# Preparing the last layers' weights inside a row scan, folding a norm into message weights, and moving stores and columns to the scalar queue

## The chip, the cores and the metric

The kernel runs on one core of a Trainium2 chip. A core has a matrix engine (TensorE, PE in the profile; PEld is its weight load), a vector engine (DVE), a scalar engine (ACT), GpSimd (POOL) and SyncE (SP), which here gives out most of the DMAs. Each engine takes its instructions in order; a DMA is given out by SP or ACT (SPq and ACTq in a timeline) and moved by the core's 16 DMA engines. The metric is device time of one execution in microseconds (us); lower is better.

## What is computed

The input is x of 4 images (b), 128 channels, 128x128 positions, all in fp32. Four layers follow each other, each as `x = x + layer(gn(x))`, with `gn` a group norm over 32 groups of 4 channels. Cut to what matters here:

```python
# layer 0: deformable 3x3 convolution, relu
x = x + relu(deform_conv(gn(x), offset))
# layer 1: scan over rows; conv1d over 9 taps of the row before
def step(carry, row):
    new = row + relu(conv1d_same(carry, W))
    return new, new
x = x + scan(step, gn(x))
# layer 2: messages along rows and columns
v = gn(x)
x = x + v @ Wself.T + (sum(v, axis=2) @ Wm.T)[:, :, None] + (sum(v, axis=1) @ Wk.T)[:, None]
# layer 3: triangle product with gates
xn = layer_norm(gn(x), norm_g, norm_b)
left = (xn @ left_w + left_b) * sigmoid(xn @ lgate_w + lgate_b)
right = (xn @ right_w + right_b) * sigmoid(xn @ rgate_w + rgate_b)
out = einsum('bkjd,bkid->bijd', left, right)
out = layer_norm(out, onorm_g, onorm_b) * sigmoid(xn @ ogate_w + ogate_b)
x = x + (out @ to_out_w + to_out_b)
```

## The kernel before

The kernel is one program of four stages. The first, `deform_layer`, is not touched by the change; it ends by writing x1 (the input of layer 1) to DRAM.

**Weights of the last layers** (`last_weights`, called ahead of the scan). Five columns, the output weights and the five matrices of layer 3 (left, right and their gates, 512 columns in all, and the output gate's 128) are loaded on ACT's queue, their biases on SP's. From them `wcat` is made: the matrices times the norm's gain (`gained`), with two matmuls for each of two pieces (512 and 128 columns), in PSUM tiles `prep_ps` and `prepb_ps` of a pool of their own, and copies by DVE (lines 1206 to 1218). After it the kernel loads the message layer's three matrices on ACT's queue.

**Scan** (`scan_layer`). Rows are handled in groups of RB = 4; the four images share each instruction where they can. For each row y and each half h of the images there are eight matmuls `both_ps` (L1099), one and eight more `own_ps` (L1104, L1110), then on ACT a copy `shared` and on DVE `total`, `carry` (the new row), `diff` and `x2c` (the row of layer 1's output). The next row's input is transposed by PE (`x1T_ps`, L1064) and normed by ACT (`rowT`). `own_ps` comes from a pool of 3 buffers. At the end of a group DVE takes statistics of `x2c` (`bn_stats`, L1144) and its sum over w (`sum_w`, L1148), POOL adds `sum_h`, and ACT's queue stores x2T. Input rows are loaded on SP (`x1rows`), the scan's own weights `wconv` on ACT's queue. Tile's scheduler orders the instructions of each engine in this and all earlier stages.

**Message terms** (`message_terms`). From the statistics come s and t, so that gn(x2) = s x2 + t. The self term is folded into one matrix per image, `ws` = wself s + identity. The sums over w and over h (128x512 for all images) are normed by four DVE operations `msg`, multiplied by wm and wk, and wself t is added by a third product; `z` of shape (2, image, 128) is the row term and the column term.

**Last layers** (`last_layers`), image by image, with an order written out by hand: `manual_schedule` keeps the instructions of each engine in the order of the program, and generators are advanced by `step`. For image b:
- `messages(b)`: for eight rows of positions at a time, `x2c` is loaded, `pair_ps` = ws x2c (L1345), `zc` = row term + column term (POOL, L1332), and X = pair_ps + zc (DVE, L1349), with statistics.
- `scaled(b)`: the scale `s` of X (L1380) and a matrix `cs`; X is stored as `x3T` in eight stores of 1 MB (L1375), for the residual at the end.
- `normed(b)`: `pair_ps` = cs X (L1435), its square `sq` on ACT (L1441), and X rewritten on ACT; from the squares `divided` makes the standard deviation, sends it through DRAM (`stdT`, `rstd`, `rwide`, all on SP's queue) and multiplies X by it.
- `multiplied(b, q)` for four quarters q of the hidden columns: left and right times their gates, the output gates stored as `gateT`, then the triangle product into `T`.
- `given_out(b)`: 32 steps k of four columns. A step loads `x3` (from x3T) and `gate` (from gateT) on SP's queue, transposes `u` (L1585), makes y on ACT (L1587), multiplies it by the gate (L1588, on POOL, and on DVE for the last image), multiplies by the output weights (L1600), and copies the sum to `x` on ACT (L1617), which SP stores. `u`, the normed column of T, is made two steps ahead: of a step's four columns three on ACT (L1615) and one on POOL (L1613); for the last image, whose output has nothing beside it, two and two.

`given_out(b-1)` is `out_of` in the main loop: its steps stand among those of image b's messages, `scaled`, `normed` and first three quarters. While it passes the three steps of `scaled` it is at k = 2, 3 and 4.

Of the kernel before, what the change touches and what calls it, by code (L numbers as in the profile page):

```python
# [10 lines left out]
F32 = mybir.dt.float32  # L11
I32 = mybir.dt.int32
BF16 = mybir.dt.bfloat16
AF = mybir.ActivationFunctionType
ALU = mybir.AluOpType
AX = mybir.AxisListType
PSUM = bass.MemoryType.PSUM
DRAM = bass.MemoryType.DRAM

P = 128  # L20
B = 4
S = 128
# [985 lines left out]
                nc.vector.tensor_copy(to, v)  # L1008


def scan_layer(tc, c, small, x1, w, norms, x2T):

# [6 lines left out]
    nc = tc.nc  # L1019
    RB = 4  # L1020
# [9 lines left out]
    with ExitStack() as ctx:  # L1030
# [54 lines left out]
        diffs = [None, None]  # L1085
        for y in range(S):
            i = y % RB
            if i == 0:
                x2c = two.tile([P, B, RB, S], F32, name="x2c")
                if y + RB < S:  # L1090
                    chunks[y + RB] = rows(y + RB)
            px, rt = ready.pop(y)
            old, new = carry[(y + 1) % 2], carry[y % 2]
            conv = []
            if y:
                for h in range(2):
                    both = ps_b.tile([P, HB, V], F32, name="both_ps")
                    for j in range(NJ):
                        nc.tensor.matmul(  # L1099
                            both, lhsT=wsum[:, j, :], rhs=old[h][:, 1, :, j : j + V],  # L1100
                            start=(j == 0), stop=(j == NJ - 1),
                        )
                    own = ps_y.tile([P, 2, HB, V], F32, name="own_ps")
                    nc.tensor.matmul(  # L1104
                        own, lhsT=wt[:, TAPS - 1, :], rhs=old[h][:, :, :, NJ : NJ + V],
                        start=True, stop=False,
                    )
                    for n in range(2):
                        for j in range(NJ):
                            nc.tensor.matmul(  # L1110
                                own[:, n], lhsT=wt[:, 2 * j + n, :],
                                rhs=diffs[h][:, n, :, j : j + V],
                                start=False, stop=(n == 1 and j == NJ - 1),
                            )
                    conv.append((both, own))
            if y + 1 < S:
                ready[y + 1] = turned(chunks[(y + 1) // RB * RB], (y + 1) % RB)
            for h in range(2):
                bs = slice(h * HB, (h + 1) * HB)
                mid = new[h][:, :, :, PAD // 2 : PAD // 2 + V]  # L1120
                if y:
                    both, own = conv[h]
                    shared = two.tile([P, HB, V], F32, name="shared")
                    nc.scalar.copy(shared, both)
                    total = two.tile([P, 2, HB, V], F32, name="total")
                    nc.vector.tensor_tensor(
                        total, own, shared.unsqueeze(1).to_broadcast([P, 2, HB, V]), ALU.add
                    )
# [12 lines left out]
            if i == RB - 1:  # L1141
                y0 = y + 1 - RB
                for b in range(B):
                    nc.vector.bn_stats(  # L1144
                        stats[:, b, y // RB, :], x2c[:, b].rearrange("p h w -> p (h w)")
                    )
                    nc.scalar.dma_start(x2T[b, :, y0 : y + 1, :], x2c[:, b])
                nc.vector.tensor_reduce(sum_w[:, :, y0 : y + 1], x2c, AX.X, ALU.add)  # L1148
                for r in range(RB):
                    nc.gpsimd.tensor_tensor(sum_h, sum_h, x2c[:, :, r], ALU.add)  # L1150
                chunks.pop(y0)
    return stats, sum_w, sum_h


def last_weights(tc, c, wp, w3):

    nc = tc.nc
    (norm_g, norm_b, left_w, left_b, right_w, right_b, lgate_w, lgate_b, rgate_w, rgate_b,
# [21 lines left out]
    NP_ = NQ * 4 * DQ + P  # L1180
    wcat = w.wcat = wp.tile([P, NP_], F32, name="wcat")
    w.gcols = slice(NQ * 4 * DQ, NP_)
    with tc.tile_pool(name="l3prep", bufs=1) as prep, tc.tile_pool(
        name="l3ps_w", bufs=2, space=PSUM
    ) as ps_w:
        raw = prep.tile([P, NP_], F32, name="wraw")
        braw = prep.tile([1, NP_], F32, name="braw")
        blocks = raw[:, 0 : NQ * 4 * DQ].rearrange("p (q n e) -> p q n e", q=NQ, n=4)
# [15 lines left out]
        nc.vector.tensor_scalar(less[0:1], less[0:1], -1.0, None, ALU.add)  # L1204
        for n0 in range(0, NP_, 512):
            n1 = min(n0 + 512, NP_)
            pw = ps_w.tile([P, 512], F32, name="prep_ps")
            nc.tensor.matmul(
                pw[:, : n1 - n0], lhsT=less, rhs=gained[:, n0:n1], start=True, stop=True
            )  # L1210
            nc.vector.tensor_copy(wcat[:, n0:n1], pw[:, : n1 - n0])
            pb = ps_w.tile([P, 512], F32, name="prepb_ps")
            nc.tensor.matmul(
                pb[:, : n1 - n0], lhsT=bwide, rhs=raw[:, n0:n1], start=True, stop=True
            )
            nc.vector.tensor_tensor(
                wcat[0:1, n0:n1], pb[0:1, : n1 - n0], braw[:, n0:n1], ALU.add
            )
    return w


def message_terms(tc, c, keep, work, counted, w2, outb):


    nc = tc.nc
    stats, sum_w, sum_h = counted
    wself, wm, wk = w2
    ws = keep.tile([P, B, P], F32, name="ws")
    z = keep.tile([P, 2, B, S], F32, name="z")
    with tc.tile_pool(name="l2ps", bufs=1, space=PSUM) as psum:  # L1230
# [15 lines left out]
        nc.vector.reciprocal(s, s)  # L1246
        t = work.tile([P, B], F32, name="t2")
        nc.vector.scalar_tensor_tensor(t, mean, -1.0, s, ALU.mult, ALU.mult)
        for b in range(B):
            nc.vector.scalar_tensor_tensor(  # L1250
                ws[:, b], wself, s[:, b : b + 1], c.ident, ALU.mult, ALU.add
            )
        tsum = work.tile([P, B], F32, name="tsum")
        nc.vector.tensor_scalar(tsum, t, float(S), None, ALU.mult)
        msg = work.tile([P, 2, B, S], F32, name="msg")
        for n, sums in enumerate((sum_w, sum_h)):
            for by, op in ((s, ALU.mult), (tsum, ALU.add)):
                nc.vector.tensor_tensor(
                    msg[:, n], sums if op is ALU.mult else msg[:, n],
                    by.unsqueeze(2).to_broadcast([P, B, S]), op,  # L1260
                )
        twide = work.tile([P, B, S], F32, name="twide")
        nc.vector.tensor_copy(twide, t.unsqueeze(2).to_broadcast([P, B, S]))
        pm = psum.tile([P, B, S], F32, name="row_ps")
        nc.tensor.matmul(pm, lhsT=wm, rhs=msg[:, 0], start=True, stop=False)
        nc.tensor.matmul(pm, lhsT=wself, rhs=twide, start=False, stop=True)
        pk = psum.tile([P, B, S], F32, name="column_ps")
        nc.tensor.matmul(pk, lhsT=wk, rhs=msg[:, 1], start=True, stop=True)

        nc.vector.tensor_scalar(z[:, 0], pm, outb, None, ALU.add)  # L1270
        nc.scalar.copy(z[:, 1], pk)
    return ws, z


def last_layers(tc, c, terms, w, x2T, out, x3T, gateT, stdT):
# [9 lines left out]
    with ExitStack() as ctx:  # L1285
# [74 lines left out]
        def scaled(b):  # L1360
# [11 lines left out]
            nc.vector.tensor_tensor(d, d, d, ALU.mult)  # L1372
            nc.vector.tensor_tensor(d, d, mv[:, 1:2], ALU.add)
            for j0 in range(0, S, 16):
                nc.sync.dma_start(x3T[b, :, j0 : j0 + 16, :], X[:, j0 : j0 + 16, :])  # L1375
# [153 lines left out]
        def given_out(b):  # L1529
# [45 lines left out]
            for k in range(-6, NS_ + 1):  # L1575
# [31 lines left out]
                if 0 <= k + 2 < NS_:  # L1607
                    u = us[k + 2] = two.tile([P, 4, P], F32, name="u")
                    for j, (r, m) in enumerate(factors.pop(k + 2)):
                        of = column(b, 4 * (k + 2) + j)  # L1610
                        to = u[:, j].rearrange("p (q d) -> p q d", q=NQ)
                        if j >= (2 if alone else 3):
                            nc.gpsimd.tensor_scalar(to, of, r, m, ALU.mult, ALU.add)  # L1613
                        else:
                            nc.scalar.activation(to, of, AF.Identity, bias=m, scale=r)  # L1615
# [62 lines left out]
def tile_preact_convs(ctx: ExitStack, tc: tile.TileContext, x, w_off, b_off, w_def, w_conv,  # L1678
# [17 lines left out]
    with tc.If(nc.values_load(far, min_val=0, max_val=1) > 0):  # L1696
        deform_general(tc, c, norms, x, w_off, b_off, w_def, x1, imgs)
    wp = ctx.enter_context(tc.tile_pool(name="l3w", bufs=1))
    w = last_weights(tc, c, wp, w3)
    with tc.tile_pool(name="l2", bufs=1) as l2:  # L1700
        w2 = []
        for v, name in ((wself_T, "wself"), (wm_T, "wm"), (wk_T, "wk")):
            t = l2.tile([P, P], F32, name=name)
            nc.scalar.dma_start(t, v)
            w2.append(t)
        counted = scan_layer(tc, c, l2, x1, w_conv, norms, x2T)
# [50 lines left out]
```

## Time and profile before

| | us |
|---|---|
| median of 3 runs | 5461.79 |
| lowest, highest | 5455.35, 5473.43 |
| the profiled execution | 5459.8 |
| its span | 5458.1 |
| first stage (to the scan's start) | 3088 |
| scan | 3088 to 3956 |
| message terms | 3956 to 3973 |
| last layers | 3973 to 5458 |

The mean granted clock of TensorE is 0.960. The stages are read from the timeline by the first and last instruction of their lines. Image 0 of the last layers takes 3973 to 4262, each later one some 360, and the last output alone, without other work, 116 us at the end.

A row of a timeline reads: start in the span, time, engine, line, operation, the tile written <- the tiles read, shape, how often in a row, and in brackets how long the engine had been idle and what ended that. SPq and ACTq are the times in which a queue's engine gave out a transfer. A row of waits reads: engine, operation and line, what it waited for, then us in total, times, and the longest. A row of the windows gives, after its length, the busy time of PE, PEld, DVE, ACT and POOL, the granted clock, the share of the DMA engines and the GB/s.

### The profile page before, as it was taken

Reading aid. Unit: us, or ns where it says so; the run is one execution under the profiler, and the core shown is the slowest. Engines: PE = TensorE matmul, PEld = TensorE weight load, DVE = VectorE, ACT = ScalarE, POOL = GpSimd, SP = SyncE. Lnnn points to the kernel's source line nnn. Section 1 sums busy time; section 2 is a strip of 40 time slices with the busy share of each in tenths; the row PEclk is TensorE's granted clock in tenths of the full one; section 3 lists DMA queues with packets and bytes.
Section 4 is the critical chain, followed back from the end, with each engine's and each line's share of the span. In section 5 each row is a group of like instructions: output and inputs, shape, how many; then the busy total and the mean of one; then the engine's idle time right before and its main releaser. Section 6 shows DMA issues by size and latency. Waiting matters only on the chain. (4 is left out here: it accounts for less than half of the span.)

```text
span 5458.1 us, 162832 instructions
## 1 busy us (share of the span) xinstructions
PE 4887.5 (90%) x68890; PEld 4229.0 (77%) x68890; DVE 3237.4 (59%) x8389; ACT 2536.8 (46%) x5206; POOL 1137.0 (21%) x1013
## 2 busy tenths in 40 slices
PE   1898999999999998989999799999969699798897
PEld 1787788788888787877899699999928478396596
DVE  4676666666666655665545466666654654546445
ACT  1554454544554444545544233333234375573666
POOL 4222121210221201212100011111120232323222
PEclk9999998999999999999999899999989899899998
DMA  5776666665666665665644322222141553554535
GB/s 151 162 161 145 138 139 140 142 150 103 142 138 130 157 120 107 150 130 126 129 85 90 73 82 78 78 84 83 61 166 64 174 179 122 195 172 145 191 132 193
DMA packets 1273817, 710.67 MB, mean 130 GB/s; under 512 B 845645, under 2 KB 1112174, under 8 KB 1263862
## 3 DMA queue, kind: packets, MB, share of 16 engines
q1 hardware_dynamic: 1243538, 658.56, 47.8%
q10 hardware_dynamic: 29540, 41.60, 2.2%
q8 instruction: 545, 8.93, 0.7%
q14 instruction: 194, 1.59, 0.1%
HBM read 417.28 MB, written 282.55 MB: 128 GB/s over the span
## 5 line engine op out<-in xcount | busy, mean ns | idle before, releaser
L606 PE MATMUL conv_ps<-ring,wdef 128*128 128x192 f32 (+2 forms) x7632 | 1301.2, 320 | 8.7 <-DVE x1c L576 6.6
L514 DVE TENSOR_TENSOR m<-t_ps,tent 128x390 f32<-128x390 f32 x1548 | 806.7, 557 | 783.2 <-ACT tent L512 767.5
L606 PEld LDWEIGHTS conv_ps<-ring,wdef 128*128 128x128 f32 x7632 | 1146.9, 195 | 127.1 <-issue 64.6
L512 ACT COPY tent<-t_ps 128x390 f32<-128x390 f32 x1560 | 690.5, 487 | 654.7 <-PE t_ps L498 642.2
L498 PE MATMUL t_ps<-parts_of,spread 57*64 57x99 bf16 (+1 forms) x12384 | 742.5, 275 | 169.0 <-DVE m L514 149.3
L523 PE MATMUL v_ps<-m,pixels 60*64 60x108 f32 (+1 forms) x22704 | 812.5, 264 | 19.0 <-DVE m L514 11.1
L498 PEld LDWEIGHTS <-spread 57*64 57x64 bf16 x12480 | 578.7, 125 | 313.0 <-issue 265.7
L523 PEld LDWEIGHTS v_ps<-m,pixels 60*64 60x64 f32 x22704 | 673.0, 137 | 69.8 <-DVE m L514 24.7
L549 ACT COPY ring<-v_ps 128x432 f32<-128x432 f32 x1032 | 505.1, 525 | 445.7 <-PE v_ps L523 444.8
L420 POOL TENSOR_TENSOR off<-off,koff 72x512 f32<-72x512 f32 x128 | 162.7, 1271 | 1768.2 <-DVE off L417 1768.2
L1500 DVE TENSOR_TENSOR T<-pair_ps,sig 128x256 f32<-128x256 f32 x512 | 282.6, 594 | 390.8 <-ACT sig L1497 390.7
L1110 PEld LDWEIGHTS own_ps<-diff,wconv 128*128 128x128 f32 x4064 | 493.6, 191 | 13.1
L1492 PEld LDWEIGHTS pair_ps<-wcat,X 128*128 128x128 f32 x4096 | 472.7, 192 | 38.1 <-issue 29.1
L1110 PE MATMUL own_ps<-diff,wconv 128*128 128x128 f32 x4064 | 494.6, 273 | 0.0
L1492 PE MATMUL pair_ps<-wcat,X 128*128 128x128 f32 x4096 | 481.5, 276 | 5.2 <-DVE T L1500 3.1
L506 PE MATMUL t_ps<-parts_of,spread 57*64 57x130 bf16 x9288 | 454.5, 225 | 0.0
L1150 POOL TENSOR_TENSOR sum_h<-sum_h,x2c 128x512 f32<-128x512 f32 x128 | 162.4, 1268 | 1150.5 <-DVE x2c L1136 684.8
L438 DVE SCALAR_TENSOR_TENSOR parts<-off,parts 72x512 bf16<-72x512 f32 x384 | 296.1, 771 | 153.5 <-ACT parts L430 147.7
L1068 ACT ACTIVATE rowT<-x1T_ps,t_x,s_x 128x128 f32<-128x128 f32 x512 | 208.2, 571 | 323.2 <-PE x1T_ps L1064 320.8
L506 PEld LDWEIGHTS <-spread 57*64 57x64 bf16 x9312 | 318.9, 108 | 0.1
L1497 ACT ACTIVATE sig<-pair_ps 128x512 f32<-128x512 f32 x256 | 152.1, 598 | 253.5 <-DVE T L1500 104.6
L1099 PE MATMUL both_ps<-carry,wsum 128*128 128x128 f32 x2032 | 268.3, 273 | 1.1 <-DVE carry L1133 1.1
(195 smaller groups left out, 6609.8 us busy)
## 6 DMA issues: line engine op xcount, KB each, us to landing
pixels<-tab SPq DMA_DIRECT2D x688, 123.8 KB
parts_of<-off SPq DMA_DIRECT2D x1032, 55.7 KB
off<-parts SPq DMA_DIRECT2D x64, 891.0 KB
tab<-rows SPq DMA_DIRECT2D x384, 128.0 KB
xin<-in_x_dram SPq DMA_DIRECT2D x128, 256.0 KB
x<-x1c SPq DMA_DIRECT2D x32, 1024.0 KB
x1rows<-x SPq DMA_DIRECT2D x128, 256.0 KB
x2T<-x2c ACTq DMA_DIRECT2D x128, 256.0 KB
```

The costliest lines, as they stand in the source:

```text
L438: nc.vector.scalar_tensor_tensor(parts[:, NSPLIT + i, h : h + RO, 2 : S + 2], off, 0.0, part, ALU.is_gt, ALU.mult,)
L498: nc.tensor.matmul(tp[h : h + HALF, 0, 0:n].rearrange("p (r c) -> p r c", c=PADW)[:, :, i:PADW:RX], lhsT=spread[0:k, kx // 2, i, h : h + H ...
L506: nc.tensor.matmul(tp[h : h + HALF, 1, i * PADW : (i + 1) * PADW], lhsT=spread[HALF : HALF + k, kx // 2, first + i, h : h + HALF], rhs=src ...
L512: nc.scalar.copy(tent[:, 0:n], tp[:, 0, 0:n])
L514: nc.vector.tensor_tensor(m, *pair, ALU.mult)
L523: nc.tensor.matmul(to[p1 : p1 + HALF], lhsT=pix[p0 : p0 + LANES, xb, :], rhs=m[p0 : p0 + LANES, :, RX * xb : RX * xb + w], start=True, sto ...
L549: nc.scalar.copy(to, bodies[side])
L606: nc.tensor.matmul(pc[:, at : at + rows, x0:x1], lhsT=wdef[:, side, k, :], rhs=v[:, :, k if v.shape[2] == NK else kx, x0 + kx : x1 + kx], ...
L1099: nc.tensor.matmul(both, lhsT=wsum[:, j, :], rhs=old[h][:, 1, :, j : j + V], start=(j == 0), stop=(j == NJ - 1),)
L1110: nc.tensor.matmul(own[:, n], lhsT=wt[:, 2 * j + n, :], rhs=diffs[h][:, n, :, j : j + V], start=False, stop=(n == 1 and j == NJ - 1),)
L1492: nc.tensor.matmul(pj[:, j], lhsT=X[:, j0 + j, :], rhs=w.wcat[:, q * 4 * DQ : (q + 1) * 4 * DQ], start=True, stop=True,)
L1500: nc.vector.tensor_tensor(to, pj[:, :, e].rearrange("p j d -> p d j"), sig[:, :, e].rearrange("p j d -> p d j"), ALU.mult,)
```

## The change

The change has four parts.

1. `last_weights` is called by the scan at row y = 8, with PSUM tiles from the scan's pool `own_ps` in place of its own pool. `message_weights`, also called there, loads the message layer's matrices and makes `shifted` = 128 (wm + wk) + wself.
2. `message_terms` scales wm (on POOL) and wk (on ACT) by each image's s in place of norming the sums, multiplies each image's sums by them, and adds the part of t by one product with `shifted`.
3. The eight stores of x3T are given out on ACT's queue, not SP's.
4. In `given_out`, the steps k < 6 of an image that is not the last have all four columns u on ACT; the last image has one on ACT and three on POOL.

```diff
@@ scan_layer
         for y in range(S):
             i = y % RB
+            if y == 2 * RB:
+                beside(ps_y, "own_ps")
@@ last_weights
-    with tc.tile_pool(name="l3prep", bufs=1) as prep, tc.tile_pool(
-        name="l3ps_w", bufs=2, space=PSUM
-    ) as ps_w:
+    with tc.tile_pool(name="l3prep", bufs=1) as prep:
...
-            pw = ps_w.tile([P, 512], F32, name="prep_ps")
+            pw = psum.tile([P, 512], F32, name="prep_ps", tag=bank)
...
-            pb = ps_w.tile([P, 512], F32, name="prepb_ps")
+            pb = psum.tile([P, 512], F32, name="prepb_ps", tag=bank)
@@
+def message_weights(tc, work, w2):
+    nc = tc.nc
+    wt = []
+    for v, name in zip(w2, ("wself", "wm", "wk")):
+        t = work.tile([P, P], F32, name=name)
+        nc.scalar.dma_start(t, v)
+        wt.append(t)
+    wself, wm, wk = wt
+    shifted = work.tile([P, P], F32, name="wshift")
+    nc.vector.tensor_tensor(shifted, wm, wk, ALU.add)
+    nc.vector.scalar_tensor_tensor(shifted, shifted, float(S), wself, ALU.mult, ALU.add)
+    return wself, wm, wk, shifted
@@ message_terms
+        same_ps = psum.tile([P, B], F32, name="same_ps")
+        nc.tensor.matmul(same_ps, lhsT=shifted, rhs=t, start=True, stop=True)
+        same = work.tile([P, B], F32, name="same")
+        nc.vector.tensor_scalar(same, same_ps, outb, None, ALU.add)
+        scaled = work.tile([P, B, 2, P], F32, name="wscaled")
         for b in range(B):
-            nc.vector.scalar_tensor_tensor(
-                ws[:, b], wself, s[:, b : b + 1], c.ident, ALU.mult, ALU.add
-            )
-        tsum = work.tile([P, B], F32, name="tsum")
-        nc.vector.tensor_scalar(tsum, t, float(S), None, ALU.mult)
-        msg = work.tile([P, 2, B, S], F32, name="msg")
-        for n, sums in enumerate((sum_w, sum_h)):
-            for by, op in ((s, ALU.mult), (tsum, ALU.add)):
-                nc.vector.tensor_tensor(
-                    msg[:, n], sums if op is ALU.mult else msg[:, n],
-                    by.unsqueeze(2).to_broadcast([P, B, S]), op,
-                )
-        twide = work.tile([P, B, S], F32, name="twide")
-        nc.vector.tensor_copy(twide, t.unsqueeze(2).to_broadcast([P, B, S]))
-        pm = psum.tile([P, B, S], F32, name="row_ps")
-        nc.tensor.matmul(pm, lhsT=wm, rhs=msg[:, 0], start=True, stop=False)
-        nc.tensor.matmul(pm, lhsT=wself, rhs=twide, start=False, stop=True)
-        pk = psum.tile([P, B, S], F32, name="column_ps")
-        nc.tensor.matmul(pk, lhsT=wk, rhs=msg[:, 1], start=True, stop=True)
-
-        nc.vector.tensor_scalar(z[:, 0], pm, outb, None, ALU.add)
-        nc.scalar.copy(z[:, 1], pk)
+            sb = s[:, b : b + 1]
+            nc.vector.scalar_tensor_tensor(ws[:, b], wself, sb, c.ident, ALU.mult, ALU.add)
+            nc.gpsimd.tensor_scalar(scaled[:, b, 0], wm, sb, None, ALU.mult)
+            nc.scalar.activation(scaled[:, b, 1], wk, AF.Copy, scale=sb)
+            pm = psum.tile([P, 2, S], F32, name="added_ps")
+            for n, sums in enumerate((sum_w, sum_h)):
+                nc.tensor.matmul(
+                    pm[:, n], lhsT=scaled[:, b, n], rhs=sums[:, b], start=True, stop=True
+                )
+            nc.vector.tensor_scalar(z[:, 0, b], pm[:, 0], same[:, b : b + 1], None, ALU.add)
+            nc.scalar.copy(z[:, 1, b], pm[:, 1])
@@ scaled
-                nc.sync.dma_start(x3T[b, :, j0 : j0 + 16, :], X[:, j0 : j0 + 16, :])
+                nc.scalar.dma_start(x3T[b, :, j0 : j0 + 16, :], X[:, j0 : j0 + 16, :])
@@ given_out
-                        if j >= (2 if alone else 3):
+                        if j >= (1 if alone else 4 if k < 6 else 3):
@@ tile_preact_convs
-    w = last_weights(tc, c, wp, w3)
...
+        def weights(psum, bank):
+            made.append(last_weights(tc, c, wp, w3, psum, bank))
+            made.append(message_weights(tc, l2, (wself_T, wm_T, wk_T)))
+
+        counted = scan_layer(tc, c, l2, x1, w_conv, norms, x2T, weights)
```

More of the change, by code (lines that the diff above doesn't have):

```diff
@@ L1008, in deform_general, with scan_layer @@
                 nc.vector.tensor_copy(to, v)
-def scan_layer(tc, c, small, x1, w, norms, x2T):
+def scan_layer(tc, c, small, x1, w, norms, x2T, beside):
     nc = tc.nc
@@ L1152, in scan_layer, with last_weights @@
     return stats, sum_w, sum_h
-def last_weights(tc, c, wp, w3):
+def last_weights(tc, c, wp, w3, psum, bank):
     nc = tc.nc
@@ L1219, in last_weights, with message_terms @@
     return w
-def message_terms(tc, c, keep, work, counted, w2, outb):
+def message_weights(tc, work, w2):
[10 more added lines that the diff above has]
+    return wself, wm, wk, shifted
+def message_terms(tc, c, keep, work, counted, wt, outb):
     nc = tc.nc
     stats, sum_w, sum_h = counted
-    wself, wm, wk = w2
+    wself, wm, wk, shifted = wt
     ws = keep.tile([P, B, P], F32, name="ws")
@@ L1698, in tile_preact_convs @@
     wp = ctx.enter_context(tc.tile_pool(name="l3w", bufs=1))
-    w = last_weights(tc, c, wp, w3)
     with tc.tile_pool(name="l2", bufs=1) as l2:
[L1701 to L1706, printed above, removed]
+        made = []
+        def weights(psum, bank):
+            made.append(last_weights(tc, c, wp, w3, psum, bank))
+            made.append(message_weights(tc, l2, (wself_T, wm_T, wk_T)))
+        counted = scan_layer(tc, c, l2, x1, w_conv, norms, x2T, weights)
+        w, w2 = made
         terms = message_terms(tc, c, wp, l2, counted, w2, w.outb)
```

## The prediction, on record before the changed kernel ran

> **What bounds the kernel now.** I read the page's totals, then its chain, then the four places that the diff touches. The sum is made against the profiled execution, 5459.8 us around a span of 5458.1, which is 2.0 under the median of the three runs (5461.8).
>
> ```profile
> PE 4887.5 (90%) x68890; PEld 4229.0 (77%) x68890; DVE 3237.4 (59%) x8389; ACT 2536.8 (46%) x5206; POOL 1137.0 (21%) x1013
> ...
> PE pair_ps L1492 7%; PE one_ps L1519 2%; PE one_ps L1508 2%; PE one_ps L1600 2%; DVE X L1349 1%; DMA rwide<-stdT 1%; PE one_ps L1585 1%; DMA gate<-gateT 1%; DVE st L1546 1%; PE one_ps L1596 1%; DVE stats L1354 1%; PE pair_ps L1435 0%; PE pair_ps L1345 0%; DVE T L1500 0%; ACT u L1615 0%
> ```
>
> TensorE is busy for 90%, and the change takes no matmuls out of the bulk. What can go is time in which PE stands still and the chain goes by something else; in it the gate loads have 1%, some 55 us. Two such places are large. First, the start of the scan (timeline):
>
> ```profile
> 3088.19 0.77 SPq L1193 DMA_DIRECT2D braw<-in_left_b_dram  x1
> 3091.95 31.07 SPq L1055 DMA_DIRECT2D x1rows<-x  x16
> 3095.88 0.39 ACTq L1039 DMA_DIRECT2D wconv<-in_w_conv_dram  x1
> 3105.18 1.53 PE L1064 MATMUL x1T_ps<-ident,x1rows 128*128 128x128 f32 x12 [0.91 <-DVE wcat L1216]
> ```
>
> Weight loads stand ahead of the scan's own on both queues; the scan's first transposes run at 3105.18. Second, each step from one image's messages to its `normed`, here that of image 1 (timeline, then the waits of 4322 to 4358):
>
> ```profile
> 4322.86 8.26 SPq L1375 DMA_DIRECT2D x3T<-X  x8
> 4333.89 1.22 SPq L1622 DMA_DIRECT2D gate<-gateT  x1
> 4348.39 1.26 POOL L1588 TENSOR_TENSOR y<-y,gate 128x512 f32<-128x512 f32 x1 [16.07 <-DMA gate<-gateT]
> 4350.24 0.47 PE L1585 MATMUL one_ps<-ident,u 128*128 128x128 f32 x1 [14.21 <-POOL u L1613]
> 4355.43 1.11 ACT L1441 ACTIVATE sq<-pair_ps,ct 128x1024 f32<-128x1024 f32 x1 [1.53 <-PE pair_ps L1435]
> ```
>
> ```profile
> POOL y L1588 <- DMA gate<-gateT: 16.1, 1, 16.1
> PE one_ps L1585 <- POOL u L1613: 14.2, 1, 14.2
> ```
>
> Eight 1 MB stores go out on SP; a gate load issued behind them takes 14.4 us to land, POOL waits, its column of `u` waits behind it, and PE waits for that column. Images 2 and 3 show the same wait (15.0, 15.9). From the last write of X to the first `sq` is 32.6, 31.9 and 32.4 us for images 1 to 3, and 9.9 for image 0, which has no output beside it.
>
> **Part 1, weights among the scan's rows.**
> *Gain.* SP gives out the rows' loads from 3088.2 instead of 3091.95, with nothing of the weights ahead of them; `wconv`, issued at 3095.88, now comes first on ACT's queue. The first rows and wconv are 1.05 + 0.59 MB, and 3094 to 3106 moves 235 to 293 GB/s in its 2 us windows: about 6 us from 3088.2 and a landing of about 1.5 make 3095.5. Transposes start 9.7 earlier (7 to 11): **-9.7**.
> *Cold clock.* The windows show 0.50 granted until 3104, then 0.83, then 1.00; the preparation's matmuls did that warming, at 1.17 us per pass of 128x512 in place of 0.43. Now the scan's rows do it, some 4 us of them at half speed, partly under DVE: **+1.5** (0 to 2.5).
> *Loads.* ACT gives out some eight weight loads among its rowT and `shared` copies, 0.4 us each, and DVE has `gained` and the message weights' sum ahead of operations of rows 1 and 2, waiting for those loads. Those share the queue with two loads already under way: **+0.3** (0 to 3).
> *Preparation at row 8.* The changed program's order puts it at a group's boundary, where DVE is fullest (timeline of a later group):
>
> ```profile
> 3182.39 1.29 DVE L1144 BATCH_NORM_STATS2 stats<-x2c 128x6 f32<-128x512 f32 x2
> 3183.59 2.27 DVE L1148 TENSOR_REDUCE sum_w<-x2c 128x16 f32<-128x2048 f32 x1
> 3185.78 0.41 DVE L1126 TENSOR_TENSOR total<-own_ps,shared 128x256 f32<-128x256 f32 x1
> ```
>
> PE gets two products of 128x512 at 0.86 us and two of 128x128 at 0.22, 2.2 us at full clock. They take `own_ps` buffers that only DVE frees, by copies of 0.69, 0.67, 0.28 and 0.27 queued around statistics (1.29) and sum (2.27); there the carry is ready 0.78 us before PE needs it. So the 1.9 us of copies delay the row that PE waits for, and the PE work can't all lie under it: 2.2 + 1.9 = **+4.1** (2.2 if the copies are hidden, 7 if a row's products also wait for a buffer).
> Sum of part 1: -3.8.
>
> **Part 2, the norm in the message weights.** Before, `t` is ready at 3963.9, DVE works to 3968 on messages of 128x512, PE makes three products, ACT ends z at 3972.7, and the pairs begin at 3972.77. After: `same` (a 128x4 product and an add, 0.7); then for each of four images ws on DVE, a scaling on POOL and one on ACT, two products of 128x128 with a reload (0.22 each, 0.5 with the fill), z on DVE and on ACT, some 0.3 each. `added_ps` is one buffer: image b+1's product waits for image b's z on ACT, so the four cycles of about 1.7 run in series, and the pairs wait for image 3: 3963.9 + 1.5 + 6.8 = 3972.2. **-0.7** (-2.5 to +1.5; if the cycle is 2.2 instead of 1.7 the part loses).
>
> **Part 3, x3T on ACT's queue, in images 1 to 3.** SP has the next output, x3 and gate loads at once. Gate loads with no such store ahead of them take 4.9 and 3.0 us in the tail (chain of waits); so POOL's y waits for no gate. In exchange ACT gives out the stores between a `copy` that ends at 4328.3 and a `y`, and everything behind them on ACT (y, u, `s`, then the first `sq`) waits. What is late next is therefore ACT: 8.2 us for eight stores, SP's time for the same (ACT's own issues are 1.3 each in the row of x2T, four in 5.13, some 10 in all). From 4328.8 the stores end at 4337; y, four u, copy, `s`, and twice more y, u, copy of the interleaved outputs, some 2.6 to 3.6 each, bring `sq` to 4348.8, 26.0 after X. The gain is 6.6, 5.9 and 6.3: **-18.8** (0 to -12 each: nothing if the gate still comes last, 12 if the issue costs ACT little).
> *Image 0.* No output to wait for; there `s` sits behind the stores: 4028.27 to 4031.9, +3.65. But the stores took all the bandwidth (420 GB/s from 4026 to 4044), and stdT, issued at 4040.41, got its rstd load out only at 4045.13, 4.7 against 1.9 us for the pair after it; on a free SP queue that is largely won back: **+0.8** (0 to 3.7).
>
> [...]
>
> **Part 4, u on ACT.** A first-quarter step has four on ACT, 0.53 more, and POOL 0.55 less. In the messages DVE is busy for 61.2 of 63 us (4262 to 4325), so POOL's relief ends no wait there; around the transitions and in normed ACT is the later one in two or three steps: **+1.0** (0 to 3). In the tail ACT loses an u (0.50), POOL gets one (0.55). A step takes 2.41 (ACT's y, two u and copy are 2.24). Then POOL is nearly full at 3 x 0.55, and DVE's y is longer beside POOL:
>
> ```profile
> 5390.63 0.97 DVE L1588 TENSOR_TENSOR y<-y,gate 128x512 f32<-128x512 f32 x1 [0.29 <-ACT y L1587]
> 5398.45 0.69 DVE L1588 TENSOR_TENSOR y<-y,gate 128x512 f32<-128x512 f32 x1 [0.93 <-DMA gate<-gateT]
> ```
>
> The DMA share of 0.7 to 0.89 leaves little to win: **0** (-4 to +4, by 0.15 in each of some 25 steps).
>
> **Sum.** -3.8 - 0.7 - 18.8 + 0.8 + 1.0 + 0 = -21.5, from 5459.8: **5438**.
>
> **Rivals.**
> *The gates are late anyway* (16%). If loads land only as the stores end, the mechanism of the 14.4 us stays and starts 5.4 to 6 later, since the stores now wait for ACT's copy: `sq` +3.7 in each of four images, so 5438 + 18.8 - 0.8 + 4 x 3.7 = 5471. Half of it (each transition gains 0 to 3) gives 5448 to 5456, and is likelier (10 of the 16). For: DMA share is 1.0 while stores move. Against: a 256 KB load needs 3 to 5 us elsewhere in a half-full stretch.
> *ACT is held while the stores move* (10%), the slower one. [...] It loses against before once issue takes 13.6 us, and by more than 0.3% from 17.7. Against: SP gave out the same eight in 8.2 while they moved for 19.6.
> *The scan keeps nothing* (8%). If the rows' start is bounded otherwise, or row 8 stalls for 10 more: about 5448.
>
> **How the numbers follow.** A measurement of this kernel can tell about 0.3%, 16.4 us, from no change, so faster means under 5443.4 and slower over 5476. The forecast has 66%: 57 under 5443.4, 9 in 5443 to 5452, by the parts' bounds. With 3 of the third rival, faster 0.60; same 9 + 13 + 5 = 0.27; slower 3 + 10 = 0.13. The range 5420 to 5464 leaves out the second rival, the hard form of the first (6) and some 4 of tails.
>
> **What would show it.** First x1T at about 3095.5 from 3088; `s` of image 0 by 8 us behind the stores' first issue; y in images 1 to 3 without a wait for gate, with ACT the one waited for, and X to `sq` at 26; stores on ACTq in 8 to 10 us; the first pair 8.4 us after `t`; a tail of 116 us after the last image's products. I am wrong if the gate's wait is still there, if ACT's issue is over 13 us, or if the scan's rows 8 and 9 lose over 10.

## The result, and the profile after

| | before | changed |
|---|---|---|
| median of 9 runs each, us | 5461.8 | 5449.0 |
| lowest to highest | 5454.8 to 5477.2 | 5437.5 to 5469.5 |
| profiled execution's span | 5458.1 | 5450.7 |

The ratio of the changed kernel to the one before is 0.9975, with a 95% interval of 0.9959 to 0.9991: about 13 us faster (5 to 22), a quarter per cent. The forecast was 5438 and the range 5420 to 5464. A quarter per cent is less than the 0.3% from which the prediction counted a kernel as faster; it gave 0.60 to faster and 0.27 to the same.

One thing has to be put right before the two profiles are compared. The first stage has the same instructions in the same order on every engine in both programs, but it ended at 3082.1 us in the profile before and at 3072.7 in the one after. The spans differ by 7.4 us and this stage by 9.4; from its end on, this profile of the changed kernel is 2.1 us longer than the one before. All times below are therefore taken as stretches between marks (`far`, the last DVE operation of the first stage, is the zero). They come from the timelines' rows, and each kernel has a second profile from the experiments. Rows are counted from 0, as y in the program, and a row ends with the last of its `carry`:

| stretch, us | before | again | changed | again |
|---|---|---|---|---|
| far (in the span) | 3082.1 | 3085.4 | 3072.7 | 3077.6 |
| far to first x1T | 23.1 | 23.3 | 12.8 | 13.1 |
| x1T to the end of row 4 | 29.9 | 29.9 | 33.8 | 33.9 |
| rows 5 to 8 | 26.6 | 26.6 | 31.0 | 31.0 |
| rows 9 to 12 | 26.6 | 26.6 | 26.0 | 26.0 |
| t to the first pair | 8.84 | 8.43 | 8.75 | 8.75 |
| first pair to image 0's last X | 50.8 | 50.8 | 52.7 | 52.7 |
| last X to first sq, image 0 | 9.9 | 9.7 | 13.6 | 13.6 |
| the same, images 1, 2, 3 | 32.6, 31.9, 32.4 | 32.8, 31.8, 32.4 | 27.7, 27.6, 28.0 | 27.6, 27.4, 28.0 |
| sq to sq end, image 0 | 47.3 | 48.1 | 45.9 | 45.9 |
| the same, images 1, 2, 3 | 48.5, 48.4, 47.7 | 48.9, 49.0, 49.6 | 49.4, 49.8, 49.3 | 49.5, 49.4, 49.0 |
| products (first to last sig), images 1, 2, 3 | 208.7, 209.0, 209.2 | 210.6, 210.4, 210.1 | 210.7, 213.2, 210.4 | 210.8, 210.8, 208.2 |
| last sig to end | 124.5 | 124.5 | 124.5 | 122.4 |
| far to end | 2375.9 | 2385.2 | 2378.0 | 2371.3 |

The stretches that a wait bounds repeat within 0.5 us. The products move by up to 2.4 between the two profiles of a kernel (and by 5 among all), `normed` by up to 2.0. In the first profile of each the granted clock is 1.00 in the products before and 0.98 to 0.99 in the changed kernel's, and 0.94 to 0.97 against 0.93 to 0.94 in these images' `normed`. The scan's steady part (rows 17 to 127) is 740.3 us in all of them.

The start of the scan in the changed kernel's timeline: the rows' loads are the first on SP, and the transposes wait for them alone, not for the weights.

```profile
3080.61 11.09 SPq L1055 DMA_DIRECT2D x1rows<-x  x12
3085.53 3.26 PE L1064 MATMUL x1T_ps<-ident,x1rows 128*128 128x128 f32 x12 [13.44 <-DMA x1rows<-x]
```

The step from messages to normed in image 1, same view:

```profile
4316.48 0.33 ACTq L1386 DMA_DIRECT2D x3T<-X  x1
...
4319.61 1.17 SPq L1591 DMA_DIRECT2D x<-x3T  x1
4319.65 11.31 ACTq L1386 DMA_DIRECT2D x3T<-X  x4
4320.89 1.15 SPq L1633 DMA_DIRECT2D gate<-gateT  x1
...
4331.06 0.78 ACT L1598 ACTIVATE y<-one_ps,obcol,ogcol 128x512 f32<-128x512 f32 x1 [11.93 <-DMA x<-x3T]
4331.91 1.27 POOL L1599 TENSOR_TENSOR y<-y,gate 128x512 f32<-128x512 f32 x1 [20.77 <-ACT y L1598]
...
4340.86 1.11 ACT L1452 ACTIVATE sq<-pair_ps,ct 128x1024 f32<-128x1024 f32 x1
```

Ahead of `sq` POOL's y no longer waits for a gate, but for ACT's y (one wait of 6.2 us for a gate is left, behind the first `sq`). ACT gave out the first six stores by 4322.2 and then stood: the seventh went out at 4327.57 and the eighth at 4330.63. By the trace these two wait until an output store and the x3 load of the row at 4319.61 have landed: the seventh store waits for semaphore 103, which the output store given out at 4319.16 last raises at 4327.55, and the eighth for 104, which the x3 load last raises at 4330.61. All transfers of the last layers, of both queues, use the same eight semaphores (100, 102 to 106, 108, 109; the eight slots of the expectation below), and a store here goes out when the transfer before it on its semaphore has landed; this is why the row of ACT's y names that load. So ACT was held for 14.5 us, not 8.2. The output store took 8.4 us to land, the x3 load 11.0 and the gate 12.8.

### The profile page after: what moved, and what is told of

Same layout as the page of the kernel before. It is cut to its first block, busy times and chain, and to the rows that moved or that the text cites. A ratio compares the mean times of both kernels' runs of the same rounds, so it can differ in the third digit from the quotient of the medians.

```text
span 5450.7 us, 162839 instructions
## 1 busy us (share of the span) xinstructions
PE 4899.9 (90%) x68902; PEld 4242.6 (78%) x68902; DVE 3233.5 (59%) x8389; ACT 2533.2 (46%) x5205; POOL 1152.8 (21%) x1025
## 5 line engine op out<-in xcount | busy, mean ns | idle before, releaser
L1503 PEld LDWEIGHTS pair_ps<-wcat,X 128*128 128x128 f32 x4096 | 480.6, 195 | 36.4 <-issue 27.6
```

Source lines behind the costliest of these rows:

```text
L1503: nc.tensor.matmul(pj[:, j], lhsT=X[:, j0 + j, :], rhs=w.wcat[:, q * 4 * DQ : (q + 1) * 4 * DQ], start=True, stop=True,)
```

## The experiments

All are edits of the changed kernel unless they say otherwise. Where a median is given, a kernel ran 6 to 11 times, and the interval is that of the ratio to the kernel before; the others ran once.

**x3t_sp: part 3 undone.**

```diff
-                nc.scalar.dma_start(x3T[b, :, j0 : j0 + 16, :], X[:, j0 : j0 + 16, :])
+                nc.sync.dma_start(x3T[b, :, j0 : j0 + 16, :], X[:, j0 : j0 + 16, :])
```

> The changed kernel with part 3 undone: the eight stores of x3T given out on SP's queue again. Theory: part 3 takes 4.9, 4.2 and 4.3 us from the stretch between the last write of X and the first sq in images 1 to 3 (27.7, 27.6, 28.1 now) and adds 3.7 in image 0 (13.6 now). Undone, these should be about 32.5 in images 1 to 3 with PE and POOL waiting for a gate load again, and about 10 in image 0: the last layers 9 to 10 us longer in those four stretches, the time about 5459. Rival: the stores' queue is worth nothing and what those stretches gain is given back by the clock later, so that the time stays within 4 us of the changed kernel's 5449.

Measured: 31.1, 30.4 and 31.6 us from X to sq, 9.7 in image 0; median 5456.0, ratio 0.9989 (0.9976 to 1.0002). Part 3 is worth 3.4, 2.8 and 3.6 us in images 1 to 3 here and costs 3.9 in image 0, part of which comes back in normed. By the medians it is worth 7 us in all, more than the rival's 4, but the intervals of the two kernels overlap. It was expected to be worth more in those images: with the stores on SP the stretch is already 1.5, 1.4 and 0.8 us shorter than in the kernel before, and the columns of u are what the two differ by there.

**prep_ahead: part 1 undone.** The weights are loaded and prepared ahead of the scan, in a pool of four buffers.

> The changed kernel with part 1 undone: the last layers' and the message layer's weights loaded and prepared ahead of the scan again (in a PSUM pool of their own), everything else as changed. Theory: the scan's first transposes start 23 us after the first stage's last operation instead of 12.8, rows 1 to 4 take 3.9 less for a warm clock, and rows 5 to 8 take 26.6 instead of 31.0; from there to the end of the scan nothing differs: the scan ends 2.6 us later. Rival: the loads and the preparation cost nothing where they stand now and part 1 is worth the whole 10.2 us at the scan's end.

Measured: transposes 24.6 us after far, x1T to the end of row 4 31.7, rows 5 to 8 26.6, the scan's end 6.0 later than in the changed kernel, where 2.6 was expected; median 5460.7, ratio 0.9995 (0.9983 to 1.0008). This is not quite the order of the kernel before: `wconv` is given out behind all the weights, at 3090.05, and PE waits 3.0 us for it at its first products, with a granted clock of 1.00. So its 31.7 does not tell what the clock costs. The timelines do; here are products of row 1 (two lines) and row 2 in the changed kernel, then the first ones of row 1 in the kernel before:

```profile
3089.88 2.08 PE L1101 MATMUL both_ps<-carry,wsum 128*128 128x128 f32 x8 [1.10 <-DVE carry L1135]
3092.60 2.90 PE L1112 MATMUL own_ps<-diff,wconv 128*128 128x128 f32 x16
3096.67 1.95 PE L1112 MATMUL own_ps<-diff,wconv 128*128 128x128 f32 x16
```

```profile
3107.83 1.16 PE L1099 MATMUL both_ps<-carry,wsum 128*128 128x128 f32 x8 [1.12 <-DVE carry L1133]
```

In the changed kernel PE has no gap from 3089.88 to the first `total` of row 1, and this takes 5.7 us for 3.5; the clock is 0.50 until 3093, 0.60 until 3095 and 1.00 from there. The transposes take 3.3 us for 1.5, 0.7 of them waits for rows still landing. Rows 2, 3 and 4 take what they took before, within 0.02 us, though the loads, `gained` and the sum stand among them. The 3.9 us that the changed kernel has more up to row 4 are the cold clock, but for those 0.7.

Against the kernel before, part 1 brings 2.2 to 2.9 us at the scan's end (both profiles of each): the 10.2 at the start are real, and three quarters are given back within twelve rows, as the theory had it and the rival did not.

**after_again** and **before_again**: the two kernels once more, for the second columns above.

> The changed kernel once more, for a second profile. Theory: the first stage, whose code the change does not touch, ends at different times in different executions (3082 before, 3073 after), by where the granted clock falls; measured from its end, all other marks repeat within 3 us. Rival: the changed program makes the first stage 9 us faster, and it ends at 3073 again, and at 3073 in every variant of the changed program.

> The kernel before, once more, for a second profile of it. Theory: the first stage ends anywhere between 3065 and 3083 in any kernel, before too, since its code is the same; measured from there, the scan's end (873.1), the first pair (890.6), and the first sq after X (9.9, 32.6, 31.9, 32.4) repeat within 0.6 us, and the end (2375.9) within 5. Rival: the first stage of the kernel before is really some 8 us longer than that of the changed one, and ends at 3080 or later again.

Measured: 5450.7 and 5472.4 us, with far at 3077.6 and 3085.4. Measured from far the waits repeat, as expected; the ends do not (2385.2 against 2375.9 for before, where 5 was expected, and 2371.3 against 2378.0 for the changed kernel, where 3 was).

**x3t_four: four stores of 2 MB.**

```diff
-            for j0 in range(0, S, 16):
-                nc.scalar.dma_start(x3T[b, :, j0 : j0 + 16, :], X[:, j0 : j0 + 16, :])
+            for j0 in range(0, S, 32):
+                nc.scalar.dma_start(x3T[b, :, j0 : j0 + 32, :], X[:, j0 : j0 + 32, :])
```

> The changed kernel with x3T stored by four transfers of 2 MB in place of eight of 1 MB, still on ACT's queue. Theory: ACT was held for 14.6 us because the seventh and eighth store waited until an output store and an x3 load, given out by SP meanwhile, had landed (they share eight completion slots); with four stores it comes to no such slot, ACT is free 7 to 9 us after the first store, and the first sq comes 5 to 6 us earlier after X in images 1 to 3 (22 instead of 27.7). Image 0 stays at about 13.6. Rival: ACT is held by the amount of data that waits in its queue; then four stores of twice the size hold it as long, 13 to 15 us, and sq stays at 27 to 28.

Measured: ACT gave out the four in 3.1 us and was free, and image 0 fell to 9.8, but X to sq was 34.9, 35.3 and 34.4; median 5466.4, ratio 1.0010 (0.9998 to 1.0021). The hold was what the theory said, yet without it, and with stores of 2 MB, the kernel gained nothing. Its timeline and waits of image 1:

```profile
4308.77 1.24 ACTq L1386 DMA_DIRECT2D x3T<-X  x1
...
4311.35 1.19 SPq L1633 DMA_DIRECT2D gate<-gateT  x1
...
4331.05 1.26 POOL L1599 TENSOR_TENSOR y<-y,gate 128x512 f32<-128x512 f32 x1 [18.39 <-DMA gate<-gateT]
```

```profile
POOL y L1599 <- DMA gate<-gateT: 19.2, 2, 18.4
ACT x L1628 <- PE one_ps L1611: 14.6, 1, 14.6
...
PE one_ps L1607 <- DMA x<-x3T: 8.3, 1, 8.3
```

The gate, given out on SP with all stores on ACT's queue, took 19.6 us to land. It was issued 4.4 us after the first store; before, on one queue, 11.0 us after it. Counted from the first store the gate lands after 24.0 us here, 25.4 before and 17.2 in the changed kernel, and `sq` comes after 31.6, 32.6 and 24.4 (on ACT the stores begin 3.3 us after X, on SP at once). The traces' DMA records show why. In two stretches in which both queues have work, about as many packets (pieces of 2, 8 or 16 KB here) of the one end as of the other, 311 and 322, 335 and 334, though they differ in size:

| stretch of the span | SP's queue | ACT's queue |
|---|---|---|
| changed, 4323.2 to 4330.6 | 311 packets, mostly 2 KB, 77 KB/us | 322 packets, mostly 8 KB, 321 KB/us |
| x3t_four, 4314.5 to 4328.0 | 335 packets, mostly 2 KB, 46 KB/us | 334 packets, mostly 16 KB, 367 KB/us |

With stores of 2 MB for 1 MB, their packets are mostly 16 KB for 8, and SP's queue moves 46 KB/us for 77. A step's output, x3 and gate are 0.79 MB: 10 us at 77 KB/us, 17 at 46. Each of the three goes beside one store: here they land at 4320.4, 4325.9 and 4330.9, within 0.8 us of the second, third and fourth store, and in the changed kernel at 4327.5, 4330.6 and 4333.7, within 0.8 us of the third, fourth and fifth. What eight stores without the hold would give was not tried.

**x3t_spread: one store at a time, on SP, some of them in normed.** A function `keep(b, j0)` stores 16 rows: one at each of the three steps of `scaled`, then in `normed` the 16 rows from j0 + 48 ahead of each `centred(j0 + JB)`, long before they are rewritten.

> The changed kernel with the stores of x3T on SP's queue again, but spread: one at each of the three steps of scaled and then one ahead of every second normed block, three blocks before the rows are rewritten. Theory from x3t_four: a load given out on SP waits for what all queues hold ahead of it on the same 16 engines (about 20 us behind 8 MB, 8 to 11 behind 6), whichever engine gave the stores out; what gained in the changed kernel is that its last two stores were held back. With 1 MB ahead of each load the gates land in 4 to 6 us, and the first sq comes 17 to 21 us after X in images 1 to 3 (27.7 now), 9.9 in image 0 (13.6 now); some of it, up to 3 us an image, is lost again where stdT's loads meet stores in normed. Last layers 20 to 30 us shorter, the time near 5425. Rival: the loads are slow there for another reason than the queued stores (the clock, the x3 loads' own pattern), and the stretch stays above 25 us.

Measured: X to sq 16.9, 16.6, 16.7, and 9.7 in image 0: the loads wait for stores, and this is right. But normed took 59.7, 59.3 and 58.8 us, 10 more each, not 3: stdT's small transfers now meet stores on the same queue (DVE waited 28.3 us for `rwide` in image 1's normed, 18.6 in the changed kernel's). Median 5448.9 instead of 5425, ratio 0.9974 (0.9961 to 0.9988): no better than the changed kernel.

**x3t_pairs: two stores at each step, all ahead of normed, on SP.**

```diff
+        def keep(b, at):
+            for j0 in range(at, at + 32, 16):
+                nc.sync.dma_start(x3T[b, :, j0 : j0 + 16, :], X[:, j0 : j0 + 16, :])
...
-            for j0 in range(0, S, 16):
-                nc.scalar.dma_start(x3T[b, :, j0 : j0 + 16, :], X[:, j0 : j0 + 16, :])
+            keep(b, 0)
             yield
...
+            keep(b, 32)
             yield
...
+            keep(b, 64)
             yield
...
             cs, ct = xs.pop(b)
+            keep(b, 96)
```

> The changed kernel with the stores of x3T on SP's queue, two at each of the three steps of scaled and the last two ahead of normed, behind the loads of the outputs' step k = 4. Theory from x3t_spread (16.9, 16.6 and 16.7 us from X to sq, but normed 9 to 10 us longer, because stdT's short loads met the late stores): with all stores given out before normed, two ahead of each step's loads, X to sq is 19 to 22 us in images 1 to 3, and normed is 49 to 50 again; image 0 stays at 9.7 with 47 to 48 after it. That is 15 to 22 us less in all than the changed kernel, measured from the first stage's end: about 2355 to 2360. Rival: the loads wait for the whole of what is given out around them in any order, X to sq is 25 or more, or normed pays for what is still under way and is 54 or more.

**before_pairs: the same edit in the kernel before, with nothing else.**

> The kernel before with the same edit and no other part of the change: stores on SP in pairs between the output's loads. Theory: the gain belongs to the order of stores and loads and not to ACT's queue or the columns of u; X to sq falls from 32.6, 31.9 and 32.4 to 19 to 22 here too, and from the first stage's end the kernel takes 30 to 36 us less than 2376 to 2385. The first stage, 3082 and 3085 us in the two profiles of before and 3065 to 3078 in eight variants of the changed kernel, has the same program everywhere; if it falls under 3078 here, chance set it; if it is 3080 or more again, it goes with something that the changed variants share.

Measured: X to sq 17.1, 17.0, 17.0 in x3t_pairs and 16.7, 16.3, 16.7 in before_pairs; normed 52.4, 53.4, 51.7 and 52.2, 53.0, 52.3; 2345.8 and 2347.4 us from far to the end, 5412.4 and 5421.8 in all (one run each). The step is shorter than the 19 to 22 expected, normed longer than the 49 to 50 and under the rival's 54. The timeline of x3t_pairs in image 1:

```profile
4303.58 0.80 SPq L1373 DMA_DIRECT2D x3T<-X  x2
4310.42 0.40 SPq L1639 DMA_DIRECT2D gate<-gateT  x1
4310.87 0.90 SPq L1373 DMA_DIRECT2D x3T<-X  x2
4311.28 1.27 POOL L1605 TENSOR_TENSOR y<-y,gate 128x512 f32<-128x512 f32 x1 [10.01 <-ACT y L1604]
4314.84 1.28 POOL L1605 TENSOR_TENSOR y<-y,gate 128x512 f32<-128x512 f32 x1 [2.29 <-ACT y L1604]
...
4320.65 1.11 ACT L1458 ACTIVATE sq<-pair_ps,ct 128x1024 f32<-128x1024 f32 x1
```

In this step no gate is waited for ahead of `sq`, and no engine is held. The kernel before gains as much by it as the changed one, 28 to 38 us from far to the end against 25 to 32: the order of stores and loads brings this, and a second queue is not needed for it. With it in both they are 1.6 us apart, less than this stretch differs between two profiles of one kernel (6.7 and 9.3): what the other parts of the change add to it does not show.

**msg_before: part 2 undone.** `message_terms` as it was.

> The changed kernel with part 2 undone: the message terms computed as before, over sums of 128x512. Theory: the four small cycles leave PE idle, so that the granted clock is 0.5 into the first pairs; undone, t to the first pair is 8.84 again (8.75 now), and the first pair to the last X of image 0 takes 50.8 us instead of 52.7: the part costs 1.8. Rival: those 1.9 us come from the moved stores or the order of loads, and the stretch stays at 52.6.

Measured: t to the first pair 8.34, pair to the last X 50.9: the theory. The part costs 2.2 us (1.8 to 2.5 against the profiles of before and before_pairs). The windows about the first pair (at 3960.6 in the changed kernel, at 3956.3 in msg_before; the granted clock stands behind POOL's busy time), first of the changed kernel, then of msg_before, and the first pairs, first of msg_before, then of the changed kernel:

```profile
3951.00:3961.00 10.00, 5.88 (x20) 4.61 (x21) 3.01 (x11) 2.60 (x9) 6.49 (x6) 0.50 0.00 0
3961.00:3971.00 10.00, 7.81 (x13) 2.81 (x13) 6.34 (x7) 0.00 (x0) 3.17 (x2) 0.80 0.37 105
```

```profile
3946.00:3956.00 10.00, 5.26 (x8) 2.29 (x8) 5.45 (x16) 0.58 (x2) 0.00 (x0) 0.57 0.00 0
3956.00:3966.00 10.00, 5.97 (x13) 2.41 (x14) 7.53 (x7) 0.27 (x1) 7.54 (x4) 1.00 0.43 119
```

```profile
3956.32 3.70 PE L1362 MATMUL pair_ps<-x2c,ws 128*128 128x512 f32 x8 [0.68 <-ACT z L1288]
```

```profile
3960.62 5.85 PE L1356 MATMUL pair_ps<-x2c,ws 128*128 128x512 f32 x8 [0.74 <-ACT z L1282]
```

With the three wide products the clock is 1.00 by the pairs; with the eight small ones it is not (0.50 from 3961 to 3964), and the same eight pair matmuls take 5.85 us for 3.70.

**u_nine: four columns on ACT up to k = 8.** `4 if k < 6` becomes `4 if k < 9`.

> The changed kernel with all four columns of u on ACT for the steps up to k = 8 instead of 5. Theory: in the changed kernel PE stands 3.2 to 4.6 us, and once more 1.2, in the first blocks of the products of images 1 to 3, for a column of u on POOL that waits behind POOL's y and a memset that waits for a DMA; with those columns on ACT both gaps go, and from the last sq to the last sig an image takes 3 to 5 us less (213 to 219 now), less 0.5 for each of three more columns on ACT. Rival: the y on POOL is as late as u, so PE waits for y in its place and the stretch stays within 1.5 us.

Measured: the largest gap of PE in the first products of image 1 fell from 3.2 us (waiting for u) to 1.7 (now for POOL's y), and the products took 207.9, 208.1 and 207.5. That is 3 us less than the changed kernel's mean, but single images reach it without the edit (207.9 in prep_ahead's image 1); inconclusive.

**u_as_before: part 4 undone.**

> The changed kernel with part 4 undone: three columns of u on ACT and one on POOL in every step of images that are not the last, two and two in the tail. Theory: the fourth column costs ACT 0.5 in each of the steps among the stores and in normed, so X to sq is 1 to 1.5 shorter (26.3 to 26.9, 27.7 now) and normed 0.5 to 1 shorter (48.5 to 49, 49.4 now) in images 1 to 3; the tail is the same within 2 us (124.5). Rival: POOL's column is waited for in these steps, and X to sq is longer than 28.

Measured: X to sq 26.9, 26.7, 27.0, normed 49.0, 48.1, 49.2, the tail 125.9. The fourth column costs 0.8 to 1.0 us before sq. In normed the difference is 0.1 to 1.6, no more than this stretch differs between the two profiles of before; that part is not shown.

**best2: what the others pointed to.** x3t_pairs with part 2 undone, `k < 9`, and the preparation at `y == 2 * RB + 2`.

> The changed kernel with four edits: the stores of x3T in pairs on SP as in x3t_pairs; message terms as before; u on ACT up to k = 8; and the weights prepared at row 10, in the middle of a group, in place of row 8. Theory: the gains add, as each lies in a stretch of its own. X to sq 17 in images 1 to 3 and normed 52 to 53; first pair to the last X of image 0 50.8; sig to sig 208 instead of 210; and away from the statistics of a group the preparation costs its 2.2 us of PE alone, so that rows 9 to 12 take 28 to 29 instead of 26.6, with 26.6 in rows 5 to 8 (31.0 at row 8). About 2337 to 2342 us from the first stage's end, and 5405 to 5415 in all. Rival for the preparation: its cost is that of the buffers it takes from the rows, anywhere, and the group takes 31 again.

Measured: median 5422.7, ratio 0.9922 (0.9906 to 0.9937): it beats both kernels. X to sq 16.8, 16.8, 16.9; pair to X 51.0; rows 5 to 8 26.6 and rows 9 to 12 29.0, so the preparation costs 2.3 us there, against 30.99 + 25.96 - 2 x 26.64 = 3.7 at row 8. It is 2339.9 from far to end, 5.9 less than x3t_pairs, though its products (210.4, 209.2, 208.6) show nothing of `k < 9`. Its total is above that of x3t_pairs' one run, because its first stage ended at 3081.7 and that one's at 3064.9.

## Why the prediction was right, and which steps were wrong

The time lies in the range and on the forecast side; the gain was 13 us for 21.5. Term by term, from the stretches of the profiles:

| step | forecast | measured |
|---|---|---|
| scan's start | -9.7 | -9.9 to -10.5 |
| cold clock in the first rows | +1.5 | about +3.9 (33.8 for 29.9; up to 0.7 of it waits for rows) |
| loads, `gained` and sum among rows 1 and 2 | +0.3 | about 0 (rows 2 to 4 as before) |
| preparation at row 8 | +4.1 | +3.7 |
| message terms | -0.7 | about +2 |
| images 1 to 3, X to sq | -18.8 | -13.6, or -16.2 without part 4 |
| image 0 | +0.8 | about +2 |
| u on ACT | +1.0 | +2.7 before sq; in normed 0 to +2, not shown |
| tail | 0 | 0 and -2.1 |

The measured terms add up to -10 to -14, inside the interval. Single stretches show them; that they are the whole of the 13 is not shown.

*Part 1* was worked out well but for the cold clock, which cost 3.9 us, past its bound of 2.5. The prediction had some 4 us of the scan's rows at half speed; the clock stayed at 0.50 to 0.60 for 9.5 us from the first transposes, through row 1, where PE had no gap. The start came out right by two errors that offset each other: the rows' loads went out 7.9 us after far, 1.8 later than reckoned, and the transposes ran 4.9 us behind them, not 7.3.

*Part 2 has the wrong sign.* The way to the pairs was 8.75 us for the 8.3 of the sum: the first product came 0.7 us after t, not 1.5, and a cycle took 2.0, not 1.7. The products were priced at what they take, but not at what they leave behind: the clock was 0.50 up to the pairs, and the pairs took 5.85 us for 3.70. The sum had such a term at the scan's start and none here.

*Part 3 was right for a reason that was only half right,* and that it gained at all is in part luck. The prediction had ACT free after 8.2 us and gates landing in 3 to 5 on a free queue. ACT was held for 14.5 us, past the 13 that the prediction gave as a sign of being wrong and the break-even of 13.6 that the second rival named, because its last two stores waited for semaphores 103 and 104, those of SP's output store and x3 load; the stores began 2.7 us earlier than reckoned (3.3 us after X, with ACT's `u` made beside the issues), and the break-even had image 0 held as well (8.2 + 21.5 / 4), where the eight stores had the eight semaphores to themselves and went out in 8.3 us. The step's loads took 11.0 and 12.8 us, not 3 to 5, and x3t_four shows that a gate can take 19.6 on its own queue, and before_pairs gains without any second queue. The first rival's mechanism is therefore the truer one: stores and loads share the DMA engines (their busy share is 1.02 from 4323 to 4331, with packets of both queues), and what was gained is a turn-taking share of 77 KB/us, where before the loads landed behind the eighth store (x3 at 4347.6, the gate at 4348.3, the store at 4345.9). That the last two stores were held back did nothing for the gate issued at 4320.89: it landed at 4333.7, before the sixth store (4335.5). Without the hold POOL's y at 4335.3 would still have waited for it, so by this estimate the hold cost at most some 2 us there; what it did for the loads of the next step stays open.

The queues took short turns: from 4323.5 to 4325 each quarter of a microsecond has 8 to 13 pieces of 2 KB and 8 to 14 of 8 KB. What the prediction left out is that, with as many packets of each queue, the share goes by packet size: in x3t_four the 2 KB packets got 46 KB/us beside 367, a ninth.

*Part 4* was priced by ACT's 0.53 in two or three steps in all. By u_as_before the column delays `sq` by 0.8 to 1.0 us in each of three images, where ACT is the engine that is waited for.

What stays open: far was 3082.1, 3085.4 and 3072.6 in the three profiles of before and before_pairs, and between 3064.9 and 3081.7 in those of the changed kernel and its variants. The program of that stage is the same, and the differences appear at scattered places where the clock drops: from 936 to 942 us of the profile before it is 0.50, over the same instructions of the changed kernel's (935.1 to 941.1) 0.81, and 4.1 us are lost about there; from 1755 to 1765 it is 0.76, for 1.00 in the changed kernel's 1750 to 1760. That chance set them is likely, but not shown: the means are 3080.0 and 3070.2. From far to end the two kernels' two profiles each differ by 5.9 us in the mean (2380.6, 2374.7), so a good part of the measured 13 may lie in the first stage.

## What to carry to other kernels

When a small load waits behind large stores, look at what is queued on all DMA engines, not at whose queue it is on (a gate took 19.6 us on a queue without stores): giving the stores out in pairs between the loads took 16 us from each step and cost some 4 in the stage behind it, where a second queue took 5 and held its engine. Before an operation with large matmuls is replaced by small ones, see what the granted clock will be for the work after it (0.50 here, and the pairs took 5.85 us for 3.70). And where a profile pair differs in a stage that was not touched, compare stretches between marks instead of spans.

## What was not expected of the hardware

- In the two stretches counted, two queues with work were served packet for packet (311 and 322, 335 and 334): 2 KB packets got 77 KB/us beside 8 KB packets and 46 KB/us beside 16 KB packets.
- Giving out a store took ACT as long for 2 MB as for 1 MB (0.33, 0.45, 0.95 and 1.24 us for the first four of 2 MB, 0.33, 0.44, 0.96 and 1.27 of 1 MB), and the issues ran beside ACT's arithmetic (its `u` from 4317.10 to 4318.67 beside the third and fourth store).
- An engine that gives out transfers was held by another engine's: ACT's seventh and eighth store waited 5.4 and 2.7 us for SP's output store and x3 load to land (semaphores 103 and 104), with work behind them.
